# Attention's value products on 32-column tiles of TensorE in place of 64-column tiles

## The chip, the cores and the metric

The kernel runs on one core of a Trainium2 chip. The metric is the device time of one execution in microseconds (us). Beside it stands a profile: one execution taken by the hardware profiler.

## What is computed

The batch has 64 graphs of 256 nodes with 512 features; all share one adjacency matrix. Two layers follow each other, each with a residual and a layernorm. Everything is fp32.

```python
# layer 0, x: (64, 256, 512)
out = deg[None, :, None] * (x @ Wi.T + b) + einsum('ij,bjo->bio', a, x @ Wj.T)
x = layernorm(x + out)
# layer 1: attention with 8 heads of 64
q, k, v = (split_heads(x @ W.T + bias) for W, bias in (q, k, v))
scores = einsum('bhqd,bhkd->bhqk', q, k) / 8, -inf where adj == 0
out = einsum('bhqk,bhkd->bhqd', softmax(scores), v)
x = layernorm(x + out @ Wo.T + bo)
```

## The kernel before

The batch is worked off in 32 groups of two graphs (NB = 2, NG = 32). The loop at L982 makes 31 passes. A pass does the attention of group g and, in between, layer 0 of group g + 1; then come the output projection of g and the projections q, k, v of g + 1. The large products use a block scheme with seven products for eight (pair_steps, L646, and l0_steps, L502). The last group has a loop of its own (L1044 to L1062).

Attention goes by pairs of heads. A group has 2 graphs with 4 pairs each, so w runs from 0 to 7. For each w:
- scores (L791) makes the transposed scores of two heads, four products with a 64-row contraction into ps. Then VectorE adds the mask (L805) into pe, ScalarE takes the exponential in place (L809), and POOL adds the two halves of the keys into pk (L812).
- values (L826) multiplies v with pe into the PSUM bank pav: for each of two key blocks kc and each of two heads j one product. The stationary operand is 64 columns of v, the moving one 256 columns of pe. Head j lands on the partitions j * 64 to j * 64 + 63. Two successive w share one bank.
- divide_two (L846), once for two w, copies pav to aoT on ScalarE (L849) and calls divide (L871). There four products with the constant ones sum pk over the keys into den, each on a 32-column tile of its own, followed by a reciprocal on VectorE (L882), an add on POOL (L883) and eight DMAs that spread the result over the partitions (L890). The division itself is a multiplication on POOL (L844), put off until multiply() is called in the next slot.

A slot of the main loop is the body for w = 2, 4, 6, and the piece after the loop for the last pair (L998 to L1007): values twice, multiply, divide_two, then the next scores, then a piece of layer 0. So a pass has four slots, and on TensorE each is: pav, den, ps (or st, the output projection, after the fourth), then products po or pa of layer 0. After the fourth slot, the list at L1008 runs the first block product of the output projection (st) and then neighbours (L566): eight products of the graph with the two parts hi and lo of mj, into pa. hi is made by ScalarE (L524), lo by POOL (L525), from what VectorE makes at L551 and L561; L485 is a transpose on VectorE that stands between them, L520 an add.

What sets the order: all matmuls are pinned to the order in which they are written (matmul, L289, with in_order, L282), and so are some steps of the other engines. The rest is put in order by a planner when the kernel is built, with its own estimate of durations. PSUM has one bank for pav, three for den, po and st (pool ps_m), two double banks for ps and pa.

Of the kernel before, what the change touches and what calls it, by code (L numbers as in the profile page):

```python
# [16 lines left out]
P = 128  # L17
# [207 lines left out]
def unshifted_path(ctx, tc, flag, x, adj, wiT, wjT, b0, wqT, bq, wkT, bk, wvT, bv, woT, bo, out):  # L225
# [18 lines left out]
    NT = N // P  # L244
    NC = D // P
    DH = 64
    R = 32
# [30 lines left out]
    def value_bank(name):  # L278
        return ps_v.tile([P, 512], F32, tag="av", name=name)


    def in_order(ins):  # L282

        tc.keep_in_program_order(ins)
# [4 lines left out]
    def matmul(*args, **kw):  # L289
        in_order(nc.tensor.matmul(*args, **kw))  # L290
# [33 lines left out]
    xT, xS, hT, hS, qT, kT, vv, aoT, oS = ({} for _ in range(9))  # L324
# [306 lines left out]
    def pair_blocks(m, tag):  # L631

        s = p1.tile([P, 4, 2, N], F32, tag=tag, name=tag)
        return left_blocks(m[:, 0:2, 0:N], m[:, 2:4, 0:N], m[:, 0:2, N:2 * N], m[:, 2:4, N:2 * N], s)
# [33 lines left out]
    def second_late(steps):  # L668
        return [steps[0], steps[2], steps[1], *steps[3:]]
# [30 lines left out]
    def qk_steps(g, store, tag, bias, diff, early=False):  # L700

        def new_store():
            store[g] = p1.tile([P, NC, NB * N], F32, tag=tag, name=tag)

        def place(i, j):
            return store[g][:, 2 * j:2 * j + 2, i * N:(i + 1) * N]

        def biased(b):
            def evict(dst, ps):
                for m in range(2):  # L710
                    nc.scalar.activation(dst[:, m, :], ps[:, m, :], AF.Identity, bias=b[:, m:m + 1], scale=1.0)
            return evict

        def last(dst, ps, addend):
            for m in range(2):
                nc.vector.scalar_tensor_tensor(dst[:, m, :], ps[:, m, :], diff[:, m:m + 1],
                                               addend[:, m, :], ALU.add, ALU.add)

        return qkv_steps(g, True, new_store, place, biased(bias), biased(diff), last, early)
# [98 lines left out]
    pavs = {}  # L818
# [7 lines left out]
    def values(g, w):  # L826
        i, pr = divmod(w, NC)
        if w == 0:
            aoT[g] = p1.tile([P, NC, NB * N], F32, tag="aoT", name="aoT")
            oS[g] = pair_blocks(aoT[g], "oS")  # L830
        pp = w % 2
        if pp == 0:
            pavs[g] = value_bank("pav").rearrange("p (r q) -> p r q", r=2)
        pe, _ = made[g, w]
        for kc in range(NT):
            for j in range(2):
                h0 = (2 * pr + j) * DH
                matmul(pavs[g][j * DH:(j + 1) * DH, pp, :], vv[g][:, i, kc, h0:h0 + DH], pe[:, j, kc, :],
                       start=(kc == 0), stop=(kc == NT - 1))

    def multiply():
        while products:
# [73 lines left out]
    def order_of(name):  # L916
        return [(name, n) for n in RIGHT]

    for g in range(-1, NG - 1):
        o, q, k, v = (order_of(name) for name in ("wo", "wq", "wk", "wv"))  # L920
# [18 lines left out]
    p, q = l0_steps(0), l0_steps(1)  # L939
# [42 lines left out]
    for g in range(NG - 1):  # L982
# [4 lines left out]
        for w in range(2, NB * NC, 2):  # L987
            values(g, w - 2)
            values(g, w - 1)
            multiply()  # L990
            divide_two(g, w - 1)
            scores(g, w)()
            if w == 4:
                run(work[2])
            later = scores(g, w + 1)
            later()
            run(work[w // 2 if w < 4 else w // 2 + 1])
        w = NB * NC - 2  # L998
        values(g, w)
        values(g, w + 1)  # L1000
        multiply()
        o = o_steps(g)
        q = second_late(qk_steps(g + 1, qT, "qT", bq_sb, bqd))
# [20 lines left out]
    g = NG - 1  # L1024
# [89 lines left out]
```

## Time and profile before

| | |
|---|---|
| median of 3 runs | 3117.25 us (3113.67 to 3117.7) |
| span of the profiled execution, first to last instruction | 3114.5 us |
| TensorE matmuls (PE) busy | 3066.7 us |
| VectorE (DVE) busy | 2200.1 us |
| POOL busy | 1505.3 us |
| ScalarE (ACT) busy | 967.4 us |
| granted TensorE clock, mean | 0.999 |

How to read it: PE is TensorE's matmuls, PEld its weight loads, which overlap them. A group of instructions reads "line, engine, operation, output<-inputs, array rows*columns, shapes, xcount", then busy time and the mean ns of one, then the idle time of the engine before them and what ended it. Almost all matmuls have the line L290, that of the helper, so one goes by the names of the tiles. The record of one matmul lasts from its start until its last result, so the records of successive matmuls overlap: the distance between their starts is what they cost. A line of the waits reads "who waits <- for whom: us in total, times, longest".

### The profile page before, as it was taken

How to read it: one execution, taken by the hardware profiler on the slowest of the kernel's cores; microseconds unless marked ns; L12 is line 12 of the kernel's file. 1: busy time of each engine (PE TensorE's matmuls, PEld its weight loads, DVE VectorE, ACT ScalarE, POOL GpSimd, SP SyncE). 2: the span in 40 equal slices, each digit the busy share in tenths (PEclk: the TensorE clock that was granted, in tenths of full speed). 3: DMA queues.
4: the chain of work that ended last, by engine and by line, in shares of the span. 5: the costliest groups of instructions: out<-in, count | busy, mean ns of one | idle time of the engine just before them, and what ended most of it. 6: DMA issues, size and time to landing. Idle time of an engine off the chain costs nothing. (4 is left out here: it accounts for less than half of the span.)

```text
span 3114.5 us, 42683 instructions
## 1 busy us (share of the span) xinstructions
PE 3066.7 (98%) x14598; PEld 2125.4 (68%) x14598; DVE 2200.1 (71%) x3298; ACT 967.4 (31%) x1861; POOL 1505.3 (48%) x1255
## 2 busy tenths in 40 slices
PE   8999999999999999999999999999999999999998
PEld 4667766677766777666776667776677766677665
DVE  6776677766777767777667776677766777767775
ACT  2322333323333323332233332333332333323332
POOL 2544445544545445454454554454543545445453
PEclk9999999999999999999999999999999999999999
DMA  7355544455444555345553445544455444555333
GB/s 253 116 151 156 166 122 131 133 155 165 143 123 125 157 165 152 117 129 151 156 166 119 129 135 158 164 142 124 124 159 164 144 123 125 158 158 158 119 106 103
DMA packets 410395, 447.28 MB, mean 144 GB/s; under 512 B 40896, under 2 KB 300224, under 8 KB 409792
## 3 DMA queue, kind: packets, MB, share of 16 engines
q1 hardware_dynamic: 410176, 444.50, 48.4%
q8 instruction: 120, 1.97, 0.3%
q14 instruction: 99, 0.81, 0.1%
HBM read 340.79 MB, written 70.25 MB: 132 GB/s over the span
## 5 line engine op out<-in xcount | busy, mean ns | idle before, releaser
L461 POOL TENSOR_TENSOR rstd<-ve,mhalf 128x1 f32<-128x1 f32 x256 | 140.4, 552 | 715.8 <-DVE below L459 715.8
L812 POOL TENSOR_TENSOR pk<-pe 128x512 f32<-128x512 f32 x256 | 322.5, 1276 | 327.6 <-ACT pe L809 327.5
L290 PE MATMUL po<-w,xS 128*128 128x512 f32 x1024 | 462.4, 599 | 0.4 <-DVE xS L478 0.4
L290 PE MATMUL st<-hS,factor 128*128 128x256 f32 x2048 | 453.5, 380 | 5.1 <-DVE xh L740 3.8
L290 PEld LDWEIGHTS st<-hS,factor 128*128 128x128 f32 x2048 | 388.9, 190 | 60.1 <-DVE xh L740 6.4
L809 ACT ACTIVATE pe<-pe 128x1024 f32<-128x1024 f32 x256 | 270.9, 1058 | 379.0 <-DVE pe L805 379.0
L290 PE MATMUL po<-w,xT 128*128 128x512 f32 x768 | 354.5, 605 | 13.1 <-DVE xT L485 11.1
L290 PE MATMUL st<-hT,factor 128*128 128x256 f32 x1536 | 352.6, 380 | 0.7 <-ACT hT L622 0.7
L290 PEld LDWEIGHTS po<-w,xS 128*128 128x128 f32 x1024 | 190.1, 191 | 235.9 <-issue 206.4
L805 DVE TENSOR_TENSOR pe<-ps,maskT 128x1024 f32<-128x1024 f32 x256 | 298.1, 1195 | 35.3 <-PE ps L290 35.3
L290 PEld LDWEIGHTS st<-hT,factor 128*128 128x128 f32 x1536 | 292.2, 190 | 41.7 <-ACT hT L622 0.9
L882 DVE RECIPROCAL rden<-den 128x256 f32<-128x256 f32 x127 | 223.1, 1757 | 92.2 <-PE den L290 89.0
L290 PEld LDWEIGHTS po<-w,xT 128*128 128x128 f32 x768 | 144.7, 192 | 181.2 <-issue 163.3
L290 PE MATMUL ps<-qT,kT 64*128 64x256 f32 x2048 | 265.0, 393 | 0.0
L290 PE MATMUL pav<-pe,v_sb 128*64 128x256 f32 x2048 | 250.2, 386 | 1.9 <-ACT pe L809 1.8
L883 POOL TENSOR_TENSOR rtot<-rtot,rden 128x256 f32<-128x256 f32 x127 | 92.3, 727 | 329.7 <-DVE rden L882 329.7
L740 DVE TENSOR_TENSOR xh<-st,xh 128x512 f32<-128x512 f32 x186 | 144.6, 777 | 136.4 <-PE st L290 136.4
L290 PEld LDWEIGHTS pav<-pe,v_sb 128*64 128x64 f32 x2048 | 135.3, 136 | 154.0 <-issue 95.4
L290 PEld LDWEIGHTS ps<-qT,kT 64*128 64x128 f32 x2048 | 184.7, 187 | 77.8 <-issue 51.3
L290 PE MATMUL st<-factor,hS 128*128 128x256 f32 x1024 | 234.8, 383 | 0.0
L525 POOL TENSOR_TENSOR lo<-mj,hi 128x512 fp32r<-128x512 f32 x128 | 175.2, 1378 | 107.3 <-ACT hi L524 107.3
L290 PE MATMUL st<-factor,oS 128*128 128x256 f32 x992 | 224.3, 380 | 0.0
(115 smaller groups left out, 4679.5 us busy)
## 6 DMA issues: line engine op xcount, KB each, us to landing
xB<-in_x_dram SPq DMA_DIRECT2D x256, 128.0 KB, 3.8
xh<-in_x_dram SPq DMA_DIRECT2D x64, 512.0 KB, 4.2
factor<-wq SPq DMA_DIRECT2D x128, 256.0 KB, 4.3
factor<-wk SPq DMA_DIRECT2D x128, 256.0 KB, 3.0
factor<-wv SPq DMA_DIRECT2D x128, 256.0 KB, 2.7
spread<-rden SPq DMA_DIRECT2D x1016, 32.0 KB, 1.9
factor<-wo SPq DMA_DIRECT2D x124, 256.0 KB, 3.2
h_cols<-xh SPq DMA_DIRECT2D x124, 256.0 KB, 2.4
```

The source lines that it names most:

```text
L290: in_order(nc.tensor.matmul(*args, **kw))
L461: nc.gpsimd.tensor_tensor(rstd, ve, mhalf, ALU.pow)
L525: nc.gpsimd.tensor_tensor(k["lo"][:, t, :], k["mj"][:, t, :], k["hi"][:, t, :].bitcast(F32), ALU.subtract)
L740: nc.vector.tensor_add(dst, src, dst)
L805: nc.vector.tensor_add(pe.rearrange("p j t q -> p j (t q)"), ps.rearrange("p j t q -> p j (t q)"), maskT.rearrange("p t q -> p (t q)").uns ...
L809: in_order(nc.scalar.activation(flat, flat, AF.Exp, scale=QSCALE, accum_out=etot[:, NB * g + i, pr:pr + 1]))
L812: nc.gpsimd.tensor_tensor(pk, pe[:, :, 0, :], pe[:, :, 1, :], ALU.add)
L882: nc.vector.reciprocal(rden, den)
L883: nc.gpsimd.tensor_tensor(rtot, rtot, rden, ALU.add)
```

## The change

In values, the inner loop over the two heads j becomes a loop over four quarters q of 32 columns. Two quarters make a head: q // 2 is the head whose pe is the moving operand. Each product takes 32 columns of v as its stationary operand, and its result lands on the partitions q * 32 to q * 32 + 31 of pav; the column tile is given by tile_position. The moving operand is still 256 columns. Nothing else is touched. R = 32 (L247) and P = 128, so q runs over four.

```diff
         for kc in range(NT):
-            for j in range(2):
-                h0 = (2 * pr + j) * DH
-                matmul(pavs[g][j * DH:(j + 1) * DH, pp, :], vv[g][:, i, kc, h0:h0 + DH], pe[:, j, kc, :],
-                       start=(kc == 0), stop=(kc == NT - 1))
+            for q in range(P // R):
+                d0 = 2 * pr * DH + q * R
+                matmul(pavs[g][q * R:(q + 1) * R, pp, :], vv[g][:, i, kc, d0:d0 + R], pe[:, q // 2, kc, :],
+                       start=(kc == 0), stop=(kc == NT - 1), tile_position=(0, q * R))
```

## The prediction

> **What bounds the kernel now.** First the page's busy times and its slices:
>
> ```profile
> span 3114.5 us, 42683 instructions
> PE 3066.7 (98%) x14598; PEld 2125.4 (68%) x14598; DVE 2200.1 (71%) x3298; ACT 967.4 (31%) x1861; POOL 1505.3 (48%) x1255
> PE   8999999999999999999999999999999999999998
> PEclk9999999999999999999999999999999999999999
> ```
>
> TensorE is busy in every slice, at full clock; the others have room. Then the waits of the matmul engine, to see whether that busy time is ever cut by somebody else:
>
> ```profile
> PE pa L290 <- POOL lo L525: 15.9, 31, 0.5
> PE po L290 <- DVE xT L485: 11.1, 2, 8.3
> PE st L290 <- DVE xh L740: 3.8, 5, 1.2
> ```
>
> There are eight smaller ones, of 2.3 us or less each. So the time is the length of TensorE's own stream, with one wait that returns in each of 31 passes. Third, the groups by form, for the changed products and for the one stretch that already uses 32-column tiles:
>
> ```profile
> L290 PE MATMUL pav<-pe,v_sb 128*64 128x256 f32 x2048 | 250.2, 386 | 1.9 <-ACT pe L809 1.8
> L290 PEld LDWEIGHTS pav<-pe,v_sb 128*64 128x64 f32 x2048 | 135.3, 136 | 154.0 <-issue 95.4
> L290 PE MATMUL den<-pk,ones 128*32 128x256 f32 x1016 | 81.8, 391 | 0.0
> L290 PEld LDWEIGHTS den<-pk,ones 128*32 128x32 f32 x1016 | 20.3, 108 | 49.2 <-issue 25.0 <-POOL pk L812 12.3 <-POOL lo L525 11.9
> ```
>
> An fp32 product stands as two records (1024 products, 2048 records). Fourth, the timeline of one of the four slots of a pass, the last one:
>
> ```profile
> 1089.24 7.13 PE L290 MATMUL po<-w,xS 128*128 128x512 f32 x16
> 1096.31 1.95 PE L290 MATMUL pav<-pe,v_sb 128*64 128x256 f32 x16
> 1098.19 0.64 PE L290 MATMUL den<-pk,ones 128*32 128x256 f32 x8
> 1098.76 2.00 PE L290 MATMUL st<-factor,aoT 128*128 128x256 f32 x8
> ...
> 1101.94 0.50 PE L290 MATMUL pa<-lo,graph 128*128 128x512 f32 x1 [0.49 <-POOL lo L525]
> ```
>
> Both values() calls of a slot (16 records) run on, then den, then another tiling. I read the starts of the single records behind these merged lines; they are the same in all 124 slots to within 2 ns, so I use them as the price list:
> - pav: starts at 0, 7 | 267, 273 | 483, 489 | 698, 705 | ... | 1562, 1568 ns. Two tiles start together, and a pair follows each 215.8 ns, but the second pair comes only after 267. The first pair lasts 431 ns, all others 379 to 380.
> - den: starts at 0, 7, 13, 20 | 240, 247, 254, 260. All four tiles start within 20 ns; the first four last 403 ns, the second four 380.
> - From the last record of one tiling to the first of the next is 309 ns (pav to den, den to ps, den to st), in place of 216: 93 ns for the change of tiling. From po, whose pace is 429 ns, it is 522: again 93.
> - The first step of a tiling is longer by 105 ns with 128 columns (320), by 51 with 64 (267), by 24 with 32 (240). It is proportional to the columns: the first load isn't hidden.
>
> **What the Trainium skill says.** "TensorEngine Tiling (Array Packing)", section Key Properties, says that changing the tiling mode drains TensorE, while tiles work independently. The trace agrees: 93 ns at each of these changes, and den's four tiles start 20 ns apart. "TensorE: Matmul & The Clock Gate", section LDWEIGHTS, gives columns/1.2 ns for a load, whatever the rows: 107, 53 and 27 ns for 128, 64 and 32 columns. The exposed 105, 51 and 24 agree. The same page, section "Part 3: Packing small matmuls", gives some 4 ns between tiles that overlap; here it is 6.5.
>
> **The change, part by part.**
> (1) The number of products. A values() call issues 8 in place of 4, a slot 16 in place of 8, so 32 records in place of 16, and as many loads. They stand four abreast where two stood: 8 steps of the array before, 8 after. If four tiles keep den's pace, the stream itself costs the same: 8 x 215.8 ns. den is the row for it: its second four last 380 ns and release the array 309 ns later, just as pav does, so four streams at once are no slower than two, over the two steps that den has. More than two steps running isn't shown. Bounds: no gain below 215.8, since the array time of a pass of 256 columns doesn't shrink; above, den's first step of 240 if that were the pace, and 432 if only two of the four overlapped. I take 215.8.
> (2) The first load: 240 - 267 = -27 ns a slot.
> (3) No change of tiling between pav and den, since both are now 128*32: -93 ns, and den's first load can go in behind running products: -24 ns.
> (4) The tail. Four tiles start over 20 ns, two over 6.5, but den had that tail anyway.
> The sum for a slot, from pav's first start to the first start after den. Before: 1568 + 309 + 260 + 309 = 2446 ns. After: ten steps, the second at 240, eight more of 215.8, then 20 to the last tile and 309: 240 + 1726 + 20 + 309 = 2295. Gain 151 ns.
>
> **Where it reaches the end.** 31 passes with four slots each. I compared the end of each producer with the start of the TensorE instruction that waits for it. The shortest such distances are 54 ns, which is a release just in time. In slots 1 to 3 den stands 543 ns or more behind its last pk, pav's second half 793 behind its exponential, the products po 764 behind VectorE. The second ps of slot 2 is 145 behind VectorE (L805), but that add starts from den's end by way of L882, so both move together. So these three slots keep their 151 ns: 93 x 0.151 = 14.0 us.
> Slot 4 is another matter. After den come 8 records of st, then pa, whose third product of j = 0 waits for POOL's lo (L525). This lo hangs on L551, which waits for the po products before pav, then L520, L485, L561 on VectorE, hi on ScalarE (L524), lo on POOL: nothing of it waits for pav or den. If these end 151 ns earlier, the wait of 0.49 becomes 0.64 and pa starts when it did. Gain 0 of 31 x 0.151 = 4.7 us; that is the other bound.
> The last group runs with values() of one pair at a time. Three times den follows directly (-0.15 each), but two waits for the exponentials (0.83 and 0.98) swallow part, and its last den has 64-column tiles, where a change of tiling appears that wasn't there: 93 + 51 ns. I take 0.2 us in all.
> Nothing is moved on another queue: no DMA, no eviction, no POOL step is added; the copy L849 and the reciprocal L882 get their banks sooner. The other engines have the same work in 0.5% less time.
> Sum: 14.0 + 0 + 0.2 = 14.2 us of the profiled span of 3114.5, so 3100.3. The median of the runs, 3117.25, is 2.75 above that span, and I carry this over: **3103.0 us**, 0.46% faster.
>
> **The rivals.**
> B, slot 4 gains too (if a changed order lets lo come earlier): 14.2 + 4.7 = 18.9, so 3098.3. Against it: the 31 equal waits of 0.5.
> C, den's 240 ns is the pace of four tiles, not a first step. A slot is then 9 x 240 + 20 + 309 = 2489, 43 ns more: 93 x 0.043 = 4.0 us, slot 4's slack taking its own, so 3121. Against it: the same lengthened first step stands in all tilings, and den's second step ends on the common 309.
> D, ends slower: **the overlap of four fails**, in the place of pav alone, where two neighbouring tiles read the same pe block (den's four read four different ones) and the stream of records per step is twice as dense for eight steps, not two. If only two overlap, pav takes 16 steps: +8 x 215.8 - 151 = 1575 ns a slot; 93 x 1.575 + 31 x (1.575 - 0.49) + some 5 in the last group = 185 us, so 3302. It decides from a pace of 235 ns on, where (2446 - 240 - 20 - 309) / 8 = 235 makes a slot as long as before. For it: eight instructions per 216 ns in place of four. Against: between two waits of PE's sequencer 125 ns apart stand the 16 loads and matmuls of a block product, so 8 in 216 ns is no limit while they are queued.
> E, the planner that orders the unpinned instructions of VectorE, ScalarE, POOL and the DMA queue prices the new products differently and moves some. One new wait of 0.3 us a pass takes 9.3 us back: 3112. For it: L805, L812, L849 and L882 are unpinned. Against: distances of 0.5 us and more nearly everywhere.
>
> **How the numbers follow.** A measurement of this kernel can tell about 0.2% (6.2 us) from no change. The forecast 0.72, B 0.05, C 0.08, D 0.07, E 0.08. Faster by over 0.2% is A and B: 0.77; within it C and E: 0.16; slower D: 0.07. The range takes in A, B and E, 0.85: 3097 to 3112. The forecast's own is 3100 to 3107.
>
> **What would show it.** Right: 4096 pav records of 128*32 with loads near 108 ns; fours starting 215.8 ns apart; pav to den 216 ns without a 93; a slot from 2446 to 2295; pa waiting for lo 31 times, near 0.64; otherwise the same waits. Wrong: pav busy near 500 us (D), steps of 235 or more (C), new entries in TensorE's waits (E), or pa's wait staying at 0.5 (B).

## The result and the profile after

| | before | after |
|---|---|---|
| median of 5 runs each | 3116.09 us (3113.67 to 3117.7) | 3102.23 us (3096.99 to 3103.52) |
| span of the profiled execution | 3114.5 us | 3101.7 us |
| ratio of the runs, 95% interval | | 0.9961 [0.9949, 0.9973] |

The ratio is the time of the changed kernel over that of the kernel before, with its 95% interval in brackets. The change makes the kernel 13.9 us (0.4%) faster, as forecast (3103.0 us, 0.46%). The page of the changed kernel, the same lines as before:

```profile
span 3101.7 us, 46779 instructions
PE 3046.5 (98%) x16646; PEld 2119.5 (68%) x16646; DVE 2202.0 (71%) x3298; ACT 967.2 (31%) x1861; POOL 1506.2 (49%) x1255
PE   7999999999999999999999999999999999999998
PEclk9999999999999999999999999999999999999999
```

2048 matmul records more, and 20 us less of busy TensorE. VectorE, ScalarE, POOL and the DMA queue have the same work; their instructions stand in the same order in both programs, one for one. The groups by form, after:

```profile
L290 PE MATMUL pav<-pe,v_sb 128*32 128x256 f32 x4096 | 248.4, 382 | 1.9 <-ACT pe L809 1.9
L290 PE MATMUL den<-pk,ones 128*32 128x256 f32 x1016 | 79.1, 379 | 0.0
L290 PEld LDWEIGHTS pav<-pe,v_sb 128*32 128x32 f32 x4096 | 119.6, 109 | 164.5 <-issue 95.5 <-ACT pe L809 3.8
L290 PEld LDWEIGHTS den<-pk,ones 128*32 128x32 f32 x1016 | 35.5, 110 | 20.3 <-POOL pk L812 0.7
```

Twice as many pav records take the same busy time (248.4 us for 250.2). The mean of a den record falls from 391 to 379 ns, its usual length in running products: its first step has no exposed load any more. den's loads are spread over a longer time (35.5 us for 20.3), since the first four now go in while pav's last products run: the first starts 214 ns ahead of den's first product, where it was 2. The fourth slot in the timeline, after:

```profile
1093.13 1.93 PE L290 MATMUL pav<-pe,v_sb 128*32 128x256 f32 x32
1094.88 0.61 PE L290 MATMUL den<-pk,ones 128*32 128x256 f32 x8
1095.42 1.99 PE L290 MATMUL st<-factor,aoT 128*128 128x256 f32 x8
...
1098.79 0.50 PE L290 MATMUL pa<-lo,graph 128*128 128x512 f32 x1 [0.68 <-POOL lo L525]
```

From pav to st it is 2.29 us where it was 2.45. The starts of the single records (in fours, of which the first is given), again the same in all 124 slots to within 2 ns: pav 0, 7, 13, 20 | 240 | 456 | 672 | 887 | 1103 | 1319 | 1535 to 1555 ns, den 196 ns after that, its own fours at 0 and 216, and 309 to the next. The sum is 1555 + 196 + 236 + 309 = 2296 ns, 150 less than 2446. And the longest waits of the matmul engine:

```profile
PE pa L290 <- POOL lo L525: 21.5, 31, 0.7
PE po L290 <- DMA w<-in_wiT_dram: 9.3, 1, 9.3
PE st L290 <- DVE xh L740: 3.8, 6, 1.0
```

pa's wait for lo grew from 15.9 to 21.5 us, by 5.6. The fourth slot's 150 ns, if they end there, account for 4.7 of them (31 x 0.150); most of the rest goes with lo itself, which in this execution ended some 20 ns later, counted from the slot's first pav product (median 5619 ns for 5601). From den's first start to the next den's first start the means of the four stretches of a pass went from 11438, 10265, 11438 and 62808 ns to 11288, 10122, 11288 and 62856: 150, 143 and 150 less, and nothing gained in the long one, which holds pa. The wait of 9.3 us for a weight is the first one of the program, long before the loop, and stood under another name before (8.3 us for VectorE's xT).

### The profile page after: what moved, and what is told of

The parts are those of the page before. It is cut to its first block, busy times and chain, and to the rows that moved or that the text cites. A ratio compares the mean times of both kernels' runs of the same rounds, so it can differ in the third digit from the quotient of the medians.

```text
span 3101.7 us, 46779 instructions
## 1 busy us (share of the span) xinstructions
PE 3046.5 (98%) x16646; PEld 2119.5 (68%) x16646; DVE 2202.0 (71%) x3298; ACT 967.2 (31%) x1861; POOL 1506.2 (49%) x1255
## 5 line engine op out<-in xcount | busy, mean ns | idle before, releaser
L461 POOL TENSOR_TENSOR rstd<-ve,mhalf 128x1 f32<-128x1 f32 x256 | 140.7, 554 | 714.8 <-DVE below L459 714.8
L805 DVE TENSOR_TENSOR pe<-ps,maskT 128x1024 f32<-128x1024 f32 x256 | 298.0, 1194 | 35.5 <-PE ps L290 35.5
L882 DVE RECIPROCAL rden<-den 128x256 f32<-128x256 f32 x127 | 223.1, 1757 | 76.9 <-PE den L290 73.8
L290 PE MATMUL pav<-pe,v_sb 128*32 128x256 f32 x4096 | 248.4, 382 | 1.9 <-ACT pe L809 1.9
L883 POOL TENSOR_TENSOR rtot<-rtot,rden 128x256 f32<-128x256 f32 x127 | 92.6, 729 | 320.2 <-DVE rden L882 320.2
L290 PEld LDWEIGHTS pav<-pe,v_sb 128*32 128x32 f32 x4096 | 119.6, 109 | 164.5 <-issue 95.5
L525 POOL TENSOR_TENSOR lo<-mj,hi 128x512 fp32r<-128x512 f32 x128 | 175.5, 1381 | 107.9 <-ACT hi L524 107.9
```

The source lines that it names most:

```text
L461: nc.gpsimd.tensor_tensor(rstd, ve, mhalf, ALU.pow)
L525: nc.gpsimd.tensor_tensor(k["lo"][:, t, :], k["mj"][:, t, :], k["hi"][:, t, :].bitcast(F32), ALU.subtract)
L805: nc.vector.tensor_add(pe.rearrange("p j t q -> p j (t q)"), ps.rearrange("p j t q -> p j (t q)"), maskT.rearrange("p t q -> p (t q)").uns ...
L882: nc.vector.reciprocal(rden, den)
L883: nc.gpsimd.tensor_tensor(rtot, rtot, rden, ALU.add)
```

## The experiments

The kernel before was measured again beside each set of them; its median was 3111 to 3112 us there, and each difference is taken against the one beside it. None of the first four changes the order of the instructions on VectorE, ScalarE, POOL or the DMA queue.

**Only the fourth slot, and only the first three.** In values, the 32-column loop stands under a condition, and the 64-column loop is kept for the rest:

```diff
+        if g < NG - 1 and w >= 6:    # second kernel: w < 6
+            (the loop over q, as in the change)
+            return
```

> 32-column tiles in the fourth slot of each pass alone, 64-column tiles everywhere else. Theory (the slot itself gets 150 ns shorter, but pa waits for POOL's lo, so the fourth slot keeps nothing): no change from the kernel before, 3116.1 us within 2; pa's waits for lo near 21 us in all in place of 15.9, pav to den 196 ns from the last to the first start in that slot. Rival (each slot keeps its gain, and other things give back a quarter of it): 31 x 0.15 = 4.7 us faster, 3111.4. Rival (the gain comes from four products abreast as such, wherever they stand): a quarter of 13.9, 3112.6.

> 32-column tiles in slots 1 to 3 of each pass alone; the fourth slot and the last group keep 64. Theory: the whole gain, 93 x 0.150 = 14.0 us, so 3102.1 us, the same as the changed kernel; pa's waits for lo stay at 15.9 us. Rival (each slot keeps the same share): three quarters of the gain, 3105.7.

Measured: the fourth slot alone 3111.59 against 3111.18 us, ratio 1.0003 [0.9994, 1.0011]; the first three 3098.83, ratio 0.9959 [0.9945, 0.9972]. First the line of the fourth slot alone, then that of the first three:

```profile
PE pa L290 <- POOL lo L525: 21.0, 31, 0.7
```

```profile
PE pa L290 <- POOL lo L525: 16.2, 31, 0.5
```

In the fourth slot the records show the same gain (pav to den 196 ns in place of 309), and the time doesn't move: what it saves stands as waiting. Both rivals fall: the fourth slot alone is not 3.5 or 4.7 us faster, for its interval allows at most 1.9. The first three carry all of it, 12.4 us here, with pa's wait all but unchanged. The interval of this second run alone (9 to 17 us) would leave room for three quarters of the gain, 10.4. The profiled executions decide it: the median time of a pass is 95.77 us before and with the fourth slot alone, 95.32 with the first three alone, and 95.35 with the whole change.

**Four abreast, or fewer changes of tiling?** In each slot one of the two values calls on 64 columns, the other on 32. The two kernels have the same products and differ in their order alone:

```diff
+        if g < NG - 1 and w % 2 == 1:    # mirror image: w % 2 == 0
+            (the loop over q, as in the change)
+            return
```

> In each slot the first values call on 64-column tiles, the second on 32 (last group all 64). As many products abreast on 32-column tiles as half of the change has, and pav's second half goes into den without a change of tiling, but the change of tiling now lies within pav. Theory (only the number of changes of tiling and the exposed first load count): 705 + 309 + 692 + 196 + 236 + 309 = 2447 ns a slot, as before, so 3116.1 us within 2. Rival (products four abreast run better in themselves, or den's earlier start is the gain): half of the gain, about 3109.

> The mirror image: in each slot the first values call on 32-column tiles, the second on 64 (last group all 64). The same products as in the run with wide first, only in the other order. Theory: one change of tiling and one exposed load more than before: 692 + 309 + 705 + 309 + 260 + 309 = 2584 ns a slot, 138 more; 93 x 0.138 = 12.8 us slower, 3128.9; the fourth slot's 138 ns go into pa's wait for lo, which falls from 0.49 to 0.35 us, 11 us in all. Rival (four abreast is what gains): half of the gain, about 3109, as with the other order.

Measured: wide then narrow 3110.48 against 3111.18 us, ratio 1.0 [0.9991, 1.0008]; narrow then wide 3123.43, ratio 1.004 [1.0026, 1.0054], 12.3 us slower. The fourth slot of the first and the third slot of the second:

```profile
1093.16 2.08 PE L290 MATMUL pav<-pe,v_sb 128*64 128x256 f32 x24
1095.06 0.61 PE L290 MATMUL den<-pk,ones 128*32 128x256 f32 x8
```

```profile
1088.44 2.08 PE L290 MATMUL pav<-pe,v_sb 128*32 128x256 f32 x24
1090.45 0.64 PE L290 MATMUL den<-pk,ones 128*32 128x256 f32 x8
```

The name of a merged line is that of its first record; both pav lines hold 8 records of 64 columns and 16 of 32. From pav to den it is 1.90 us in one order and 2.01 in the other, and den itself lasts 0.61 or 0.64: in the second order the tiling changes between pav and den as well. So the same products gain nothing in one order and lose 12.3 us in the other. Here four abreast is worth nothing in itself; what counts is how often the tiling changes and how many columns the first load has. The mirror image also shows the fourth slot's wait from the other side:

```profile
PE pa L290 <- POOL lo L525: 11.1, 31, 0.4
```

A longer slot shortens it by what it costs (15.9 - 11.1 = 4.8 us, 31 x 0.155), as forecast (11).

**Taking the wait for lo away.** In the list at L1008, o, q and k hold the block products of the output projection, of the queries and of the keys; take adds pa and starts a layernorm, give applies it, send writes its result out. pa goes behind one more block product, in the changed kernel (narrow, with 32-column tiles) and in the kernel before (wide, with 64):

```diff
-        run([o[0], neighbours, take1, take0, q[0], give1, send1, o[1], k[0], give0, send0, multiply,
+        run([o[0], q[0], neighbours, take1, take0, give1, send1, o[1], k[0], give0, send0, multiply,
```

> The changed kernel, with the graph products (pa) of the fourth slot put one block product later: q[0] (8 records, 1.7 us) stands ahead of neighbours in the list at L1008. Theory (the fourth slot's gain is lost only in pa's wait for lo): the wait of 21.5 us goes, since lo is 0.7 us late and q[0] covers 1.7; 21 us faster than the changed kernel, that is 34 us under the kernel before, ratio 0.989, unless take and give, which now start 1.1 us later, make somebody else late. Rival (another resource ends the pass, the wait for lo stands beside it): as the changed kernel, 0.996.

> The kernel before (64-column tiles), with the same move of neighbours behind q[0]. Theory: 15.9 us of waiting go, ratio 0.995; and the distance to the run with narrow tiles and the same move is that of all four slots, 124 x 0.150 + 0.2 = 18.8 us, in place of the 13.9 that the change brought where pa waited for lo. Rival (the fourth slot's gain is lost to something else than this wait): the distance stays near 14 us.

Measured: narrow 3089.97 against 3112.18 us, ratio 0.993 [0.9916, 0.9943]; wide 3104.62, ratio 0.9975 [0.9965, 0.9984]. Both are faster, but by 22.2 and 7.6 us in place of some 34 and 16, and the distance is 14.7 us, not 18.8. On that number the rival holds: the fourth slot's gain is still lost, though pa's returning wait for lo is gone. The waits of the narrow kernel, then of the wide one:

```profile
PE st L290 <- ACT u L711: 14.7, 31, 0.5
PE pa L290 <- POOL lo L525: 0.6, 1, 0.6
```

```profile
PE st L290 <- ACT u L711: 9.7, 31, 0.3
```

A new wait took its place, that of the block product k[1], and it is 5.0 us longer with narrow tiles (31 x 0.16), the fourth slot's 150 ns once more. The timeline of the narrow kernel says where it comes from:

```profile
1000.00 2.36 POOL L747 TENSOR_TENSOR xh<-xh,u 128x1024 f32<-128x1024 f32 x1
1002.31 0.55 POOL L461 TENSOR_TENSOR rstd<-ve,mhalf 128x1 f32<-128x1 f32 x1
1002.90 0.29 ACT L466 ACTIVATE shift<-below,rstd 128x1 f32<-128x1 f32 x1 [4.73 <-DVE st L453]
1003.22 0.81 ACT L467 ACTIVATE xh<-xh,shift,rstd 128x512 f32<-128x512 f32 x1
1003.94 0.82 ACT L711 ACTIVATE u<-st,bk 128x256 f32<-128x256 f32 x2
1004.81 1.13 PE L290 MATMUL st<-hT,factor 128*128 128x256 f32 x4 [0.47 <-ACT u L711]
```

L711, on which k[1] waits, stands behind L466 and L467 on ScalarE. These wait for L461, which stands behind L747 on POOL, and POOL has run without a gap since lo (L525, L844, L883, L746, L747). The profile puts the wait of L466 down to VectorE's L453, because that ended some 13 ns after L461. It isn't the cause: L466 does not read its result, and in the wide kernel, where that step was done 2.1 us before it, L466 starts 33 ns after L461 as it does here, in all 31 passes. So the wait still hangs on lo, along another road, and lo hangs on the products before pav. Hence the next pair: give1 and send1 behind o[1] and k[0], which puts L711 ahead of L466.

```diff
-        run([o[0], neighbours, take1, take0, q[0], give1, send1, o[1], k[0], give0, send0, multiply,
+        run([o[0], q[0], neighbours, take1, take0, o[1], k[0], give1, send1, give0, send0, multiply,
```

> The changed kernel with pa behind q[0], as in the run before last, and with give1 and send1 moved behind o[1] and k[0] too. Theory (the move of pa took the wait for lo away, but then k[1] waited 31 x 0.47 us for L711, which stood on ScalarE behind give's L466, which waited for POOL's L461 behind L747, a queue that begins with lo): L711 is now ahead of give, the 14.7 us go, and no wait of TensorE returns in each pass; 3112.2 - 22.2 - 14.5 = 3075.5, ratio 0.988. Rival (ScalarE or POOL just finds another product to hold up): as the run before, 0.993.

> The kernel before (64-column tiles) with the same two moves. Theory: its 9.7 us of waiting for L711 go as well, 3112.2 - 7.6 - 9.5 = 3095, ratio 0.9945; and since no wait is left that takes the fourth slot's gain, the distance to the run with narrow tiles is that of all four slots, 124 x 0.150 + 0.2 = 18.8 us. Rival (the fourth slot never gains): 14 us.

> The changed kernel itself once more, beside the two others on the same chip: 13 us faster than the kernel before, ratio 0.996.

Measured: narrow 3068.09 against 3111.85 us, ratio 0.986 [0.9844, 0.9875]; wide 3087.48, ratio 0.9923 [0.9909, 0.9937]; the change itself 3099.23, ratio 0.9961 [0.9947, 0.9975]. The longest waits of the narrow kernel:

```profile
PE po L290 <- DVE xT L485: 11.4, 2, 8.6
PE pt_h L293 <- ACT xh L467: 2.3, 2, 1.2
PE pav L290 <- ACT pe L809: 1.9, 3, 1.0
```

and the longest of the wide one:

```profile
PE po L290 <- DVE xT L485: 10.9, 2, 8.1
```

No wait returns 31 times any more in either, and the distance of the two kernels is 19.4 us, where 124 slots of 150 ns and 0.2 make 18.8. The median time of a pass says the same without the start and the end of the program:

| order of the program | wide | narrow | difference |
|---|---|---|---|
| as in the case | 95.77 us | 95.35 us | 0.42 |
| pa later | 95.58 us | 95.13 us | 0.44 |
| pa and give later | 95.00 us | 94.39 us | 0.61 |

Three slots' gain is 0.45 us, four slots' 0.60. In the last order the fourth slot keeps its gain. The narrow one is faster than both kernels of the case: 1.4% under the kernel before, 31 us under the change. The two moves make most of that: without narrow tiles they bring 24.4 us. Both came out 7 us below the forecast; the section on what was not expected says why.

## Why the prediction was right

By its own steps, against the profiled executions:
- **The stream costs the same** (part 1): behind a first step of 240 ns, fours start 215 to 216 ns apart through pav's eight steps and on through den's two. The bound of two den steps that I could see before carried over to ten. Rivals C (a pace of 240) and D (only two overlap) fall by these starts, and by pav's busy time.
- **The first load** (part 2): 240 for 267, as taken from den.
- **No change of tiling between pav and den** (part 3): 196 ns from the last start to the first (216 less the 20 of the stagger), den's second four after 216, not 240. The two mixed orders confirm parts 2 and 3 by time. The Trainium skill, "TensorEngine Tiling (Array Packing)", section Key Properties, says that a change of the tiling mode drains TensorE; the traces agree in that the change from pav to den cost 93 ns beyond the usual step, and these are gone. Whether it is the draining that fills them, no run shows.
- **The slot**: forecast 151 ns, measured 150: 93 for the change of tiling, 27 for pav's smaller first load, 24 for den's hidden one, and 6 because den no longer starts behind the stagger of pav's last pair.
- **Slot 4 gains nothing**: forecast a wait of 0.64 us, measured 21.5 / 31 = 0.69. (Of hi, lo, hi, lo it is pa's fourth product that waits, not the third.) That nothing is gained is shown by the runs with the fourth slot alone and with the other three alone. Rival B falls for this order of the program. That the gain isn't lost for good but only for as long as something that hangs on lo is late is shown by the last pair.
- **The distances to the producers** were misread in two places, without harm. In the third slot den stood 302 ns behind its last pk, not 543 (that is about the distance of its second four); den now comes 126 earlier, and at least 174 are left. And the shortest distance is not 54: po of slots 1 and 3 starts 32 ns after the reciprocal L882. This one starts from den's end, so it moved along.
- **Rival E** (the planner moves something) falls: the other engines' instructions have the same order.
- **The last group**: forecast 0.2 us of gain, which did not come. Of the three den that were to gain 0.15 us each only the first did (from pav's first start to the first start after den, 1583 ns became 1432); the other two stayed (1902 and 1905 became 1913 and 1910). From the loop's last den to the end of the program it is longer with narrow tiles in each order, by 0.8, 0.6 and 0.4 us. The output product po waits there for the division (POOL aoT, L844) by 0.4 to 0.9 us longer. Why the division comes later was not followed up.
- **The sum**: forecast 14.2 us. The profiled spans differ by 12.8, the medians by 13.9, and when both were measured again (the last run) by 12.6. That 13.9 lies so near 14.2 is luck: its interval goes from 8 to 16 us. The 31 passes give 31 x (150 + 143 + 150) = 13.7 and in this execution lose 30 x 48 ns = 1.4 in the long stretch, where I had put zero; the rest is 1.3 less ahead of the first den and 0.8 more behind the last. The 48 ns are no property of the change: in the second profiled execution of the same kernel that stretch is 47 ns shorter than before, not longer. Its mean scatters with a few long passes; its medians are 62.63 us before, 62.65 and 62.64 after.

## What to carry to other kernels

Where TensorE never rests, read the starts of single records at the seams, the places where one tiling follows another. Here fp32 products with 256 moving columns could be split from 64-column over 32-column tiles at no cost in the stream, and so share the tiling of their neighbour. What was gained is the seam (93 ns and an exposed load), and a smaller first load (27 ns), not the number of tiles abreast. Then ask for each place what arrives next: a gain ahead of a wait that returns in each pass became waiting here, in whatever queue the late producer held up. When such a wait is moved away, follow the producer's whole queue (here POOL's after lo), or it comes back under another name.

## What was not expected

**A wait costs more than the profile lists as idle.** In the kernel with pa later, k[1]'s wait is listed with 0.47 us. The starts of its records are 854 ns apart where 216 is usual, and the next step takes 320 where 216 is usual: 638 + 104 = 742 ns a pass. 0.16 of that is the modelled end of the record before the wait (380 ns from its start, while its successor could have started at 216), and 0.10 is a first load that nothing hides, as after a change of tiling. From that kernel to the one with give later, the long stretch of a pass fell from a median of 62440 ns to 61698: by 742. In the wide pair it fell by 578, where 0.31 was listed. Likewise pa's wait in the changed kernel, listed with 0.68, is a start 1085 ns after the one before and a next step of 334, where 231 is usual: 957 ns a pass (854 + 103), 29.7 us in all. Taking it away with no successor brought 31.1 (3099.23 to 3068.09). That is why the last pair came out better than forecast from the listed waits.

**The part of a wait that follows the producer can be passed on.** Moving pa removed 31 waits of 0.7 us and made 31 of 0.5 in another engine's name, both set by the same chain on VectorE, ScalarE and POOL.
